# Spreading the rows of B over the partitions by transfers and a ScalarE copy instead of by TensorE

## The chip, the cores and the metric

The kernel runs on one core of one Trainium2 chip. The core has five engines that work side by side[...]: TensorE (PE, the matrix multiplies), VectorE (DVE), ScalarE (ACT), GpSimd (POOL) and SyncE (SP), which here issues nearly all transfers. Transfers move data between the HBM and the on-chip memory SBUF; matmuls write to PSUM, which VectorE and ScalarE can read and write[...]. The metric is the device time of one execution in microseconds (us), the median over runs; less is better.

## What is computed

The input is a batch of four images of 48 x 48 positions with 128 channels. Layer 0 normalizes, projects to 256 inner channels, convolves, and runs four selective scans over the 2304 positions (row order, column order, and both reversed). Layer 1 is an attention followed by a spectral convolution (called STU below). Only the scan matters for the change:

```python
def step(h, inp):
    dt_l, u_l, B_l, C_l = inp
    dA = jnp.exp(dt_l[..., None] * A)
    h = h * dA + (dt_l * u_l)[..., None] * B_l[:, :, None, :]
    y = jnp.einsum('bkdn,bkn->bkd', h, C_l)
    return (h, y)
```

The state `h` has 256 channels times 16 state entries for each image and direction. `B_l` and `C_l` are 16 numbers for each position, the same for all channels: whoever forms the product `(dt*u)*B` on the chip needs each row of B repeated on all the partitions that hold a channel of that state entry.

## The kernel before, in words

**Stages.** A prologue prepares image 0. Then, for each image, comes a scan stage, and after it an epilogue with the attention, in which the next image's prologue is done as well. The STU of image b-1 runs inside the scan stage of image b, as TensorE work between the pieces of the scan; in the scan stage of image 0 there is no such STU, and the mixing of its weights (`mixture`) takes its place. The STU of the last image runs alone at the end.

**The scan stage.** Four directions k times six chunks of 384 positions (`CS`) make 24 chunks for each image. A chunk has eight units `(h, q)`: h is one of two halves of the channels, q one of four groups of four state entries. A unit is laid out as 128 partitions (four state entries times 32 channels) by four channel groups by 384 positions. For each unit:

- `spread` (L439) makes the rows of B stand on all 128 partitions, 32 partitions for each of the four state entries.
- `enter` (L445) multiplies `dt*u` by them: one instruction over 128 x 1536 elements. Three of eight units (`POOLED`, L484) do this on GpSimd, the other five on VectorE.
- `scan` (L452), four times: ScalarE computes `exp` into a PSUM tile `dA` (two buffers), VectorE scans with it.
- `times_c` (L461): GpSimd multiplies by C, and `sum_c` (L469) sums over the state entries by TensorE; `add_y` (L478) adds to the result on VectorE.

**Two ways to spread B before the change.** A unit on VectorE has its B made by a matmul of the chunk's `xd` (which holds the projected rows of B) with a constant matrix `spread` of zeros and ones, into the one PSUM tile of pool `psB` (tag "B"). A unit on GpSimd[...] its B comes to SBUF by `Chunk.fetch` (L423): four transfers of 48 KB, each reading one row of B from HBM (`xdd`) for 32 partitions. The rows of C come in the same way (fetch indices 4 to 7). `FETCHED` (L489) lists the fetched indices: 1, 3 and 4 to 7. Each fetched index has one SBUF buffer `bc`, which is refilled for the next chunk by `refill` (L542) once the second half (h = 1) of the current chunk has read it.

**Order of the work.** The order is written out by hand: `scans` (L509) emits, for each unit s, the instructions of all engines, and each engine executes its own in that order. Within step s the order is: `enter` (which multiplies for unit s+1 on VectorE or unit s+2 on GpSimd), preparation of later chunks, scan of group 0, STU or mixing work, `times_c` of unit s-1, scan of group 1, preparation, STU work, `spread(s + 2)`, scan of group 2, STU work, preparation, scan of group 3, refills, `sum_c` of unit s-2, STU work. `more` hands out the STU work in proportion to the matmul columns done so far (`done`), out of a total in which `CHUNK_COLS` (L491) are counted for each chunk of the scan.

**Preparation of a chunk** (`prep`, L342) starts 17 units before the chunk and also uses the tile "B" of `psB` for its matmuls (`xp` L368, `dt` L380); ScalarE reads those results at L373 and L383. Its softplus (L391) needs another table of functions than `exp`, so ScalarE loads a table before it and another one after it. It falls in the step of the last unit of a chunk (s mod 8 = 7), just before `spread(s + 2)`.

**The STU** multiplies at L969 (`cv`), copies one result in three to SBUF on ScalarE (`Q`, L983), adds the others to it on VectorE (`U`, L994) and multiplies by weights at L1031 (`pr`). Its Toeplitz tiles `tt` are fetched at L942.

Of the kernel before, what the change touches and what calls it, by code (L numbers as in the profile page):

```python
# [8 lines left out]
F32 = mybir.dt.float32  # L9
AF = mybir.ActivationFunctionType  # L10
ALU = mybir.AluOpType
# [4 lines left out]
P = 128  # L16
# [5 lines left out]
CS = 384  # L22
SUB = 384
NT = L // P
G4, DL, C4, Q4 = 4, 32, 4, 4
# [29 lines left out]
def hybrid_kernel(ctx: ExitStack, tc: tile.TileContext, a: dict, out: bass.AP):  # L55
# [3 lines left out]
    nc = tc.nc  # L59
    ctx.enter_context(tc.manual_schedule())  # L60
    wp = ctx.enter_context(tc.tile_pool(name="w", bufs=1, side="left"))
# [30 lines left out]
    for h in range(NH):  # L92
# [14 lines left out]
                            fill=0.0, base=0, channel_multiplier=1)  # L107
    nc.gpsimd.affine_select(gmean, gmean, pattern=[[4, C // 4], [0, 4]], compare_op=ALU.is_ge,
                            fill=0.0, base=3, channel_multiplier=-1)
# [5 lines left out]

    onerow = wp.tile([P, 1], F32, name="onerow")
    nc.vector.memset(onerow, 0.0)

    spread = wp.tile([P, 2, Q4, C4, DL], F32, name="spread")
    nc.vector.memset(spread, 0.0)  # L120
    for v in range(2):
        nc.gpsimd.affine_select(onerow, onerow, pattern=[[0, 1]], compare_op=ALU.not_equal, fill=1.0,
                                base=-R - 64 * v, channel_multiplier=1)
        nc.gpsimd.affine_select(spread[:, v], spread[:, v], pattern=[[-C4, Q4], [-1, C4], [0, DL]],
                                compare_op=ALU.not_equal, fill=1.0, base=-32 - 64 * v, channel_multiplier=1)

    csum = wp.tile([P, DL], F32, name="csum")
    nc.vector.tensor_reduce(csum, ident.rearrange("p (c j) -> p j c", j=DL), AX.X, ALU.add)
# [302 lines left out]
    class Unit:  # L431
# [7 lines left out]
        def spread(self, ps):  # L439

            self.bt = ps.tile([P, 512], F32, tag="B", name=f"B{self.name}")
            nc.tensor.matmul(self.bt[:, :CS], spread[:, self.ch.k // 2, self.q].rearrange("p c j -> p (c j)"),  # L442
                             self.ch.xd, start=True, stop=True)

        def enter(self, pool):  # L445

# [37 lines left out]
    POOLED = ((0, 3), (1, 1), (1, 3))  # L484
    order = [(k, c) for k in range(K) for c in (range(NCH) if k < 2 else reversed(range(NCH)))]
    quads = [(h, q) for h in range(NH) for q in range(Q4)]
    STEPS = 15
    LEAD = 17
    FETCHED = sorted({q for h, q in POOLED} | set(range(Q4, 2 * Q4)))  # L489

    CHUNK_COLS = (len(quads) - len(POOLED)) * CS + len(quads) * CS + 3 * CS  # L491

    def begin_scans(b, pool):

        chunks = [Chunk(b, k, c) for k, c in order]
        preps = [ch.prep(pool) for ch in chunks]
        for i in range(3 * STEPS):
            if next(preps[0]) is not None:
                yield
        for i in FETCHED:  # L500
            chunks[0].fetch(i, pool)
        for i in range(3 * (LEAD - len(quads))):
            if next(preps[1]) is not None:
                yield
        for i in range(3 * (LEAD - 2 * len(quads))):
            next(preps[2])
        yield chunks, preps

    def scans(b, chunks, preps, front, sp, back, work, work_cols):  # L509

        units = [Unit(ch, h, q) for ch in chunks for h, q in quads]
        total = len(chunks) * CHUNK_COLS + work_cols
        done = [0]

        def more(share):

            while done[0] < share * total:
                cols = next(work, None)
                if cols is None:
                    break  # L520
                done[0] += cols

        def enter(s):

            if s + 2 < len(units) and units[s + 2].pool:
                units[s + 2].enter(sp.s)
            if 0 <= s + 1 < len(units) and not units[s + 1].pool:
                units[s + 1].enter(sp.s)

        def spread(s):  # L530
            if s < len(units) and not units[s].pool:
                units[s].spread(back.psB)
                done[0] += CS

        def prepare(s):

            ci, j = divmod(s, len(quads))
            for c in range(ci + 1, ci + 4):
                if c < len(chunks) and 0 <= s - len(quads) * c + LEAD < STEPS:
                    done[0] += next(preps[c]) or 0  # L540

        def refill(s, i):  # L542

            if 0 <= s < len(units) and s // len(quads) + 1 < len(chunks):
                u, nxt = units[s], chunks[s // len(quads) + 1]
                if u.h == NH - 1:
                    nxt.fetch(i + u.q, front)

        pending = []
        spread(0)  # L550
        enter(-2)
        enter(-1)
        spread(1)
        for s in range(len(units) + 2):
            real = s < len(units)
            enter(s)
            prepare(s)
            if real:
                units[s].scan(0, back.psa)
            more((s + 0.25) / len(units))  # L560
            if 1 <= s <= len(units):
                units[s - 1].times_c()
            if real:
                units[s].scan(1, back.psa)
            if pending:
                pending.pop().add_y()
            prepare(s)
            more((s + 0.5) / len(units))
            spread(s + 2)
            if real:  # L570
                units[s].scan(2, back.psa)
            more((s + 0.75) / len(units))
            prepare(s)
            if real:
                units[s].scan(3, back.psa)
            refill(s - 3, Q4)
            if s + 1 < len(units) and units[s + 1].pool:
                refill(s + 1, 0)
            if s >= 2:
                units[s - 2].sum_c(back.psy)  # L580
                done[0] += CS
                if units[s - 2].q == Q4 - 1:
                    pending.append(units[s - 2])
            more((s + 1) / len(units))
        for u in pending:
            u.add_y()
        assert next(work, None) is None
# [528 lines left out]
    once.close()  # L1116
    front = Stage(tc, "f0", "left", one=(1, SB), xd=(3, SB), rep=(3, SB))
    first = begun(begin_scans(0, front))
    begin0.close()
    start_y(0)  # L1120
    for b in range(B):
# [3 lines left out]
        if b == 0:  # L1125
            mixed = Stage(tc, "m", "right", two=(2, SB))
            scans(b, *first, front, sp, ps, mixture(mixed, ps), MIX_COLS)
            mixed.close()
        else:
            scans(b, *first, front, sp, ps, stu_alone(b - 1, ps), STU_COLS)  # L1130
# [29 lines left out]
        if more:  # L1160
            front = Stage(tc, f"f{b + 1}", "left", one=(1, SB), xd=(3, SB), rep=(3, SB))
            pieces = begin_scans(b + 1, front)
# [67 lines left out]
```

## Time and profile before

Time before: 6410.29 us, the median of three runs from 6404.66 to 6411.98 us. The profiled execution spans 6421.2 us.

| Engine | busy, us | share of the span | instructions |
|---|---|---|---|
| PE | 5440.6 | 85% | 25032 |
| DVE | 4823.6 | 75% | 6193 |
| POOL | 3842.7 | 60% | 1825 |
| ACT | 2800.0 | 44% | 5053 |

The first queue of transfers (q1) moved 1025.00 MB. The instructions that the change touches, from the profile's groups:

| Line, engine | what | count | busy, us | mean, ns |
|---|---|---|---|---|
| L442 PE | matmul into B (two passes each) | 960 | 443.0 | 546 |
| L450 DVE | multiply by B from PSUM | 480 | 832.2 | 1734 |
| L450 POOL | multiply by B from SBUF | 288 | 994.2 | 3452 |
| L455 ACT | exp into dA | 3072 | 1782.0 | 585 |
| L429 SP | transfers of rows of B and C, 48.0 KB each | 2304 | 3.4 to landing | |

How to read it: a share of the span is an average over stages that have different limits. The part of the profile that divides the span into 40 slices shows the four scan stages as the stretches in which VectorE's digit is 9. A wait is given with the engine and the line that ended it. Idle time of an engine that doesn't set the end costs nothing.

### The profile page before, as it was taken

To read this page: it belongs to the slowest core of one execution; us is meant where nothing else is said; L and a number is where in the kernel's file an instruction comes from. 1 tells how busy PE (TensorE), PEld (TensorE's weight loads), DVE (VectorE), ACT (ScalarE), POOL (GpSimd) and SP (SyncE) were. 2 spreads that over 40 slices of the span, in tenths; PEclk is the share of its full clock that TensorE was granted. 3 is DMA by queue.
4 is the path that set the end of the run, shared out by engine and by line. 5 is a ranking of instruction groups with operands and counts; after the bars stand their busy time and mean duration, and the time that the engine had idled before them with its cause. 6 is when DMAs were issued, how large, how long until landed. Compare 5 with 4: busy or idle time off the path is not lost.

```text
span 6421.2 us, 75575 instructions
## 1 busy us (share of the span) xinstructions
PE 5440.6 (85%) x25032; PEld 3353.1 (52%) x25032; DVE 4823.6 (75%) x6193; ACT 2800.0 (44%) x5053; POOL 3842.7 (60%) x1825
## 2 busy tenths in 40 slices
PE   3656555697999998888999999788999999789999
PEld 1222222444556566544556567544555567547789
DVE  6999999548999998558999998458999999322111
ACT  2555555244555554244555554244555554221000
POOL 1989888406778887306788887207788888100000
PEclk6787777799999999899999999899999999899999
DMA  4556566126878889127878889127788888025546
GB/s 104 139 138 151 139 144 148 40 55 162 199 196 215 216 221 247 59 62 165 198 195 217 222 218 256 39 64 179 189 203 215 219 224 246 28 67 151 154 141 212
DMA packets 658246, 1033.52 MB, mean 161 GB/s; under 512 B 93856, under 2 KB 515872, under 8 KB 633120
## 3 DMA queue, kind: packets, MB, share of 16 engines
q1 hardware_dynamic: 652032, 1025.00, 62.3%
q10 hardware_dynamic: 5824, 3.69, 0.3%
q8 instruction: 200, 3.28, 0.2%
q14 instruction: 190, 1.56, 0.1%
HBM read 905.79 MB, written 122.56 MB: 160 GB/s over the span
## 4 chain that ended last, share of the span: by engine, by line
PE 45%; DVE 24%; DMA 16%; POOL 4%; issue 4%; ACT 4%; SPq 3%; DVEq 0%; ACTq 0%; POOLq 0%
PE cv L969 19%; DVE s L458 11%; PE pr L1031 6%; DVE s L450 5%; DMA tt<-fd 5%; DMA rep<-dtdud 4%; PE s L714 4%; PE y L475 3%; PE o L707 3%; DMA bc<-xdd 3%; POOL s L467 3%; PE op L650 2%; PE B L442 2%; DVE xc L264 2%; DVE re L408 2%
## 5 line engine op out<-in xcount | busy, mean ns | idle before, releaser
L467 POOL TENSOR_TENSOR s<-s,bc 128x1536 f32<-128x1536 f32 x768 | 2647.8, 3449 | 179.8 <-DVE s L458 88.9
L458 DVE TENSOR_TENSOR_SCAN s<-dA,carry,s 128x384 f32<-128x384 f32 x2560 | 2458.1, 1000 | 190.1 <-ACT dA L455 189.0
L455 ACT ACTIVATE dA<-rep,A 128x384 f32<-128x384 f32 x3072 | 1782.0, 585 | 1627.0 <-DVE s L458 1622.2
L969 PE MATMUL cv<-tt,u 128*128 128x256 f32 (+3 forms) x7680 | 1632.6, 351 | 64.3 <-DVE U L994 38.0
L969 PEld LDWEIGHTS cv<-tt,u 128*128 128x128 f32 x7680 | 1259.7, 190 | 583.1 <-issue 266.1
L450 POOL TENSOR_TENSOR s<-rep,bc 128x1536 f32<-128x1536 f32 x288 | 994.2, 3452 | 95.3 <-DMA bc<-xdd 95.3
L969 PE MATMUL cv<-tt,us 128*128 128x256 f32 (+3 forms) x3840 | 841.0, 358 | 106.6 <-DVE U L994 55.3
L994 DVE TENSOR_TENSOR U<-cv,Q 128x256 f32<-128x256 f32 (+1 forms) x1280 | 480.3, 381 | 596.0 <-PE cv L969 581.2
L450 DVE TENSOR_TENSOR s<-rep,B 128x1536 f32<-128x1536 f32 x480 | 832.2, 1734 | 56.1 <-PE B L442 32.8
L475 PE MATMUL y<-s,csum 128*32 128x384 f32 x6144 | 720.6, 544 | 142.4 <-DVE ya L481 85.0
L969 PEld LDWEIGHTS cv<-tt,us 128*128 128x128 f32 x3840 | 639.7, 195 | 323.8 <-DVE U L994 89.7
L1031 PE MATMUL pr<-U,G 128*128 128x512 f32 (+4 forms) x2048 | 694.7, 469 | 3.5 <-DVE U L994 3.2
L983 ACT COPY Q<-cv 128x256 f32<-128x256 f32 (+3 forms) x640 | 224.0, 351 | 1027.2 <-PE cv L969 1025.5
L442 PE MATMUL B<-xd,spread 128*128 128x384 f32 x960 | 443.0, 546 | 177.4 <-DVE s L450 166.8
L458 DVE TENSOR_TENSOR_SCAN s<-dA,s 128x384 f32<-128x384 f32 x512 | 459.3, 938 | 70.9 <-ACT dA L455 70.7
L466 POOL COPY carry<-s 128x4 f32<-128x4 f32 x640 | 121.6, 190 | 574.8 <-DVE s L458 534.5
L1031 PEld LDWEIGHTS pr<-U,G 128*128 128x128 f32 x2048 | 334.5, 190 | 198.2 <-issue 137.0
L714 PE MATMUL s<-xnT 128*128 128x512 f32 (+1 forms) x720 | 357.9, 582 | 42.7 <-ACT xnT L676 23.4
L475 PEld LDWEIGHTS y<-s,csum 128*32 128x32 f32 x6144 | 127.7, 112 | 497.4 <-issue 336.3
L158 POOL TENSOR_TENSOR ln_vu<-ln_vu,mhalf 128x4 f32<-128x4 f32 (+1 forms) x20 | 26.8, 1341 | 602.0 <-DVE ln_vu L157 602.0
L716 ACT ACTIVATE e<-s,shift 128x512 f32<-128x512 f32 (+1 forms) x360 | 231.2, 644 | 314.1 <-PE s L714 313.6
L707 PE MATMUL o<-e,xn 128*128 128x512 f32 (+1 forms) x720 | 343.4, 560 | 4.5 <-ACT e L716 4.5
(157 smaller groups left out, 3638.1 us busy)
## 6 DMA issues: line engine op xcount, KB each, us to landing
rep<-dtdud SPq DMA_DIRECT2D x768, 384.0 KB, 7.8
tt<-fd SPq DMA_DIRECT2D x192, 577.0 KB, 5.5
bc<-xdd SPq DMA_DIRECT2D x2304, 48.0 KB, 3.4
tt<-fd SPq DMA_DIRECT2D x192, 513.0 KB, 4.5
tt<-fd SPq DMA_DIRECT2D x192, 385.0 KB, 4.3
dtdud<-re SPq DMA_DIRECT2D x768, 96.0 KB, 2.3
G<-gd SPq DMA_DIRECT2D x192, 256.0 KB, 5.3
tt<-fd SPq DMA_DIRECT2D x64, 514.0 KB, 5.6
```

The costliest lines, as they stand in the source:

```text
L442: nc.tensor.matmul(self.bt[:, :CS], spread[:, self.ch.k // 2, self.q].rearrange("p c j -> p (c j)"), self.ch.xd, start=True, stop=True)
L450: eng.tensor_tensor(s, self.ch.rep[self.h][:, 1], bt.unsqueeze(1).to_broadcast([P, G4, CS]), ALU.mult)
L455: nc.scalar.activation(dA[:, :CS], ch.rep[self.h][:, 0, g], AF.Exp, scale=A[:, ch.k, self.h * G4 + g, self.q:self.q + 1])
L458: nc.vector.tensor_tensor_scan(s, dA[:, CS - 1::-1] if ch.rev else dA[:, :CS], s, 0.0 if ch.first else carry[:, self.h, self.q, g:g + 1], ...
L467: nc.gpsimd.tensor_tensor(self.s, self.s, ch.bc[Q4 + self.q].unsqueeze(1).to_broadcast([P, G4, CS]), ALU.mult)
L475: nc.tensor.matmul(ch.y[g * DL:(g + 1) * DL, :CS], csum, self.s[:, g], start=(self.q == 0), stop=(self.q == Q4 - 1))
L707: nc.tensor.matmul(po[J][:, :w], xn[:, i], e[:, :w], start=(i == 0), stop=(i == NT - 1))
L714: nc.tensor.matmul(p[:, :w], xnT[:, i * P:(i + 1) * P], xnT[:, 512 * J:512 * J + w], start=True, stop=True)
L716: nc.scalar.activation(e[:, :w], p[:, :w], AF.Exp, bias=shift)
L969: nc.tensor.matmul(p2[:, :, at - first:], x, t[:, :, hi - 1 - at + J * P:end if end >= 0 else None:-1], start=(J == 0), stop=(J == nb - 1))
L994: nc.vector.tensor_tensor(dst, src, q, ALU.add)
L1031: nc.tensor.matmul(p[:, :, :v], Gs[n][:, q, x, :], U[n][:, 4 * q:4 * q + 4, :v], start=False, stop=(k == KF - 1 and q == 1 and v == w))
```

## The change

The five units in eight that multiply on VectorE no longer get their B from TensorE. All four groups of rows of B are fetched by transfers (fetch indices 0 to 7 instead of 1 and 3 to 7), and ScalarE copies the fetched tile from SBUF to the PSUM tile "B", from which VectorE multiplies as before. The copy stands in the order where the matmul stood. The constant matrix `spread` goes. The refill of a row group of B is emitted in every step (it acts only for units with h = 1), no longer only before a unit of GpSimd, and the columns of the spreading matmuls are taken out of the count by which the STU work is handed out. The purpose is to take the spreading off TensorE, which also carries the STU.

```diff
-    spread = wp.tile([P, 2, Q4, C4, DL], F32, name="spread")
-    nc.vector.memset(spread, 0.0)
...
-        nc.gpsimd.affine_select(spread[:, v], spread[:, v], pattern=[[-C4, Q4], [-1, C4], [0, DL]],
-                                compare_op=ALU.not_equal, fill=1.0, base=-32 - 64 * v, channel_multiplier=1)
...
         def spread(self, ps):
 
             self.bt = ps.tile([P, 512], F32, tag="B", name=f"B{self.name}")
-            nc.tensor.matmul(self.bt[:, :CS], spread[:, self.ch.k // 2, self.q].rearrange("p c j -> p (c j)"),
-                             self.ch.xd, start=True, stop=True)
+            nc.scalar.copy(self.bt[:, :CS], self.ch.bc[self.q])
...
-    FETCHED = sorted({q for h, q in POOLED} | set(range(Q4, 2 * Q4)))
-
-    CHUNK_COLS = (len(quads) - len(POOLED)) * CS + len(quads) * CS + 3 * CS
+
+    CHUNK_COLS = len(quads) * CS + 3 * CS
...
-        for i in FETCHED:
+        for i in range(2 * Q4):
             chunks[0].fetch(i, pool)
...
                 units[s].spread(back.psB)
-                done[0] += CS
...
             refill(s - 3, Q4)
-            if s + 1 < len(units) and units[s + 1].pool:
-                refill(s + 1, 0)
+            refill(s + 1, 0)
```

## The prediction

> **What bounds the kernel now.** I read the 40 slices first. VectorE is at 9 in four stretches, the scan stages; TensorE is at 9 in the last three of them too, and the transfers' row at 7 to 9.
>
> ```profile
> PE   3656555697999998888999999788999999789999
> DVE  6999999548999998558999998458999999322111
> DMA  4556566126878889127878889127788888025546
> ```
>
> Only the scan stages hold what changes, so I asked for the busy time by window: the first scan stage and the second, from first scan to last (the third and fourth are 1127.5 and 1128.6 us), then the second cut at the starts of its chunks 8, 20 and 23. Columns: length, then busy time of PE, PEld, DVE, ACT, POOL, granted TensorE clock, share and rate of transfers.
>
> ```profile
> 124.78:1168.17 1043.39, 614.05 (x2652) 245.49 (x2652) 949.49 (x978) 597.30 (x1078) 923.42 (x423) 0.77 0.59 141
> 1471.49:2605.32 1133.83, 1047.89 (x5347) 662.26 (x5347) 1054.13 (x1303) 584.19 (x1051) 925.79 (x422) 0.98 0.83 209
> ...
> 1471.50:1872.70 401.20, 362.93 (x1586) 204.95 (x1586) 361.92 (x462) 204.57 (x374) 305.94 (x143) 0.97 0.79 190
> 1872.70:2406.10 533.40, 511.16 (x2480) 319.91 (x2480) 520.69 (x620) 292.14 (x510) 465.96 (x213) 0.99 0.86 217
> 2406.10:2563.10 157.00, 136.94 (x986) 108.58 (x987) 131.60 (x171) 68.59 (x130) 117.36 (x58) 0.93 0.92 244
> ```
>
> In the first stage VectorE is 91% busy and TensorE 59%. In the others both are at 92 to 93%, but not evenly: in the middle twelve chunks VectorE works 98% of the time, in the first eight both have 10% idle, and in chunks 20 to 22 the transfers are at 0.92. The change takes nothing from VectorE, so it can win only VectorE's idle time: 94 us in the first stage (1043.4 - 949.5), 80 in the second (1133.8 - 1054.1), 74 and 73 in the others. The lists of waits by window say what ends it. First stage, then the first eight chunks of the second, then its middle twelve (us in total, times, longest):
>
> ```profile
> DVE s L458 <- ACT dA L455: 66.3, 42, 16.4
> DVE s L450 <- PE B L442: 15.3, 7, 3.4
> DVE s L450 <- issue: 12.6, 4, 4.5
> ...
> ACT Q L983 <- PE cv L969: 75.5, 53, 9.5
> DVE s L458 <- ACT dA L455: 35.8, 31, 3.5
> ...
> DVE s L458 <- ACT dA L455: 11.3, 17, 1.5
> ```
>
> The first stage waits for B itself. (The four "issue" waits stand before the same multiply; the timeline shows one at 430.04, TensorE having stood 6.8 us for the weights `M` with the B matmul queued behind.) Later VectorE waits for `dA`, hence for ScalarE. Following each such gap back through ScalarE's records: in the first eight chunks ScalarE was mostly late from standing at a `Q` copy whose `cv` TensorE had not finished (some 25 of the 36 us); most of the rest lies behind the table loads around softplus.
>
> **What the Trainium skill says.** "ScalarE: Activation LUTs", section "What ACT_TABLE_LOAD costs", gives 186 ns + 0.833 ns per element for an instruction with immediate operands; for 384 elements an estimate of 506 ns. The trace has 472 ns for the copy of the same shape out of PSUM (L383). The page's 1283 ns for a table load is the trace's figure exactly. "DMA: Bandwidth & Descriptors", section "Issuing engines are not separate DMA queues", says that all transfers share 16 engines; so the added ones compete with `tt` and `rep`, and the 0.92 above shows where. "TensorE: Matmul & The Clock Gate", Part 1, says idle windows lower the clock: in this trace 0.77 at 59% busy against 0.98 at 92%. Lighter TensorE work may thus be paced a little slower.
>
> **The change part by part.**
>
> *TensorE loses the B matmuls*: 443.0 us over 480, so 0.92 us each and 111 us per stage. TensorE in stages two to four falls from 1048 to 937 us. This is worth time only where VectorE waited for TensorE. First stage: 26 us of B waits within the stage (15.3 + 12.6, less 1.7 before the first scan) go. First eight chunks of each later stage: 25 + 3 us (direct waits for `cv`) hang on TensorE. Five matmuls a chunk take 8 x 5 x 0.92 = 37 us from its 363, so it is nearer 85% busy than 90%; the middle chunks run well with TensorE at 96%, so I take 20 of the 28 as won. Middle: 1 us. Chunks 20 to 22 wait for transfers: 2 us.
>
> *ScalarE gains 480 copies*. Bounds are 472 ns (L383) and 585 ns (the `exp` of the same shape from SBUF to PSUM); I take 472, since no pointer operand is read. That is 57 us per stage, 584 to 641 of some 1125: no new bound, but ScalarE works in order, and behind the copy stand the `exp` of groups 2 and 3, for which VectorE waits. The copy needs its row group landed and the tile "B" read by the multiply of unit s+1. That multiply precedes the scan of group 0, whose end the next `exp` awaits anyway, so the second wait is normally covered. I laid a copy of 472 ns, record by record, into the gap before the third `exp` of each unit concerned (118 a stage), starting after ScalarE's previous record and that multiply. What the slack before the scan doesn't take up is 15.6, 18.0, 17.8 and 18.0 us by stage (22 to 23 with 600 ns). Most of it is certain: in the step of softplus the copy lies in an already late chain, here ScalarE's, then VectorE's record:
>
> ```profile
> 1567.19 1.28 ACT L391 ACT_TABLE_LOAD   x1
> 1568.48 0.84 ACT L391 ACTIVATE re<-re 128x768 f32<-128x768 f32 x1
> ...
> 1571.06 1.28 ACT L455 ACT_TABLE_LOAD   x1
> 1572.35 0.58 ACT L455 ACTIVATE dA<-rep,A 128x384 f32<-128x384 f32 x1
> ...
> 1572.97 1.02 DVE L458 TENSOR_TENSOR_SCAN s<-dA,carry,s 128x384 f32<-128x384 f32 x1 [1.63 <-ACT dA L455]
> ```
>
> 24 such steps at up to 0.47 make 11 us a stage. Of the second stage's 18, 9 fall in the first eight chunks (where an earlier `cv` gives back a third: I count 6), 8 in the middle, 2 in the end.
>
> *Transfers gain* two row groups of four transfers in each of 96 chunks: 768 of 48 KB, 37.7 MB on 1033.5. SyncE issues eight more per chunk at 0.42 us, 3.4 of some 47. The row group is fetched three steps (some 17 us) before its copy, against 3.4 us median and 13.7 at most to landing; the row group of unit 3 has the same lead today and GpSimd waited for it only at the start. So the landing costs nothing later. At the end of a stage, 24 x 49 KB = 1.2 MB at 244 GB/s would cost 4.8 us where the transfers are full; I count 3.
>
> *Start of the first stage*: the first B is now behind the `rep` transfers. In the timeline VectorE multiplies at 119.6 and GpSimd's row group lands at 129.8; a delay of 8 us, of which a gap of 16.4 us at 149.96 (TensorE waiting for `M`) takes some: 4.
>
> *Edits at nothing*: the constant `spread` and its fills lie in the prologue beside the loading of weights. Removing the columns from the count leaves the STU's mean pace as it was, hidden behind VectorE.
>
> Sum: first stage -26 + 16 + 4 = -6. Later stages: first eight chunks -20 + 6 = -14; middle -1 + 8 = +7, less 2 for copies that a `U` add on VectorE covers, +5; end -2 + 2 + 3 = +3, less 2 where a `cv` wait takes the copy in; together some -8, three times -24. In all -30: 6380 us.
>
> **The rivals.**
>
> *VectorE becomes the sole bound.* If all waits for TensorE go, the first eight chunks fall to VectorE's 362 us + 10 behind tables + 4 for copies = 376, -25; with +6 in the middle and nothing at the end, -19 a stage, -57; the first stage -25. 6328 us. For: the middle's 98%. Against: waits for a first `tt` stay.
>
> *ScalarE's copies take the place of the waits (slower).* If lighter TensorE work wins nothing in the later stages, the 69 us of copies (15.6 + 18.0 + 17.8 + 18.0), 14 for transfers (3 x 4.8), and 4 at the start stand against 26: +61, 6471 us. For: a stall of VectorE in the middle is lost for good. Against: the 25 us behind `cv` in the first eight chunks.
>
> *The two cancel*: won and lost some 60 us each, 6405 us, within 0.2%.
>
> **How the numbers follow.** The likeliest case, 6380, has 0.52; VectorE sole bound 0.14; cancelling 0.13; slower 0.21. Faster by over 0.2% (12.8 us): 0.14 + 0.47 of the first, 0.61. Same: 0.13 + 0.05, 0.18. Slower: 0.21. The range runs from 6310, below the second case since the shift of STU pieces may move each later stage by some us, to 6450, where half of the slower case is out.
>
> **What would show it.** Right: the B waits of the first stage gone; the first eight chunks of a later stage 10 to 20 us shorter with TensorE near 85%; the middle 4 to 8 us longer; the gap after softplus 0.4 us longer; chunks 20 to 22 unchanged or a little longer. Wrong: copies that wait for `bc` transfers, the middle longer by over 15 us, or the first eight chunks unmoved.

## The result, and the profile after

| | median, us | lowest to highest | runs |
|---|---|---|---|
| before | 6407.48 | 6402.20 to 6411.98 | 4 |
| after | 6465.19 | 6459.20 to 6476.28 | 4 |

The ratio is 1.0092, 95% interval 1.0075 to 1.0110: the change costs 58 us, where 30 us of gain were predicted.

The 40 slices of the kernel after, in the rows that were shown of before:

```profile
PE   3555555788988988788988888788988888789999
DVE  6999999458999998458999997459999998322111
DMA  4666666027888889128888888127878888025546
```

In the scan stages of images 1 to 3 TensorE is now mostly at 8, where it was at 9, and the transfers went from 7 to 8 in some slices. VectorE's row is hardly changed, as it has the same work. The windows of the four scan stages, first scan to last (length; busy time of PE, PEld, DVE, ACT, POOL; clock; share and rate of transfers):

```profile
130.71:1156.08 1025.37, 550.11 (x2416) 215.94 (x2416) 949.57 (x977) 642.17 (x1197) 922.11 (x423) 0.67 0.62 152
1456.39:2604.76 1148.37, 997.61 (x5109) 628.35 (x5109) 1054.23 (x1303) 631.39 (x1170) 924.64 (x422) 0.95 0.85 215
2903.45:4054.76 1151.31, 1005.50 (x5110) 634.44 (x5111) 1053.79 (x1303) 631.34 (x1170) 924.82 (x422) 0.94 0.85 214
4354.30:5506.77 1152.47, 1004.51 (x5110) 632.59 (x5111) 1052.86 (x1303) 630.86 (x1170) 924.87 (x422) 0.94 0.84 214
```

Against before the first stage is 18 us shorter (1043.4 to 1025.4), the others 15, 24 and 24 us longer (from 1133.8, 1127.5 and 1128.6), the first scan is 6 us later. VectorE's busy time is within 3 us of before in every stage, so nearly all of it is idle time: in the second stage 94 us in place of 80. (These windows are of the two profiled executions, whose spans are 41 us apart; the one of before is a longer one, so the timed 58 us is the better figure of the whole.)

The second stage cut as before, at the starts of its chunks 8 and 20:

```profile
1456.39:1856.40 400.01, 349.11 (x1510) 192.43 (x1510) 361.49 (x463) 222.00 (x415) 305.92 (x143) 0.95 0.82 200
1856.40:2399.70 543.30, 484.52 (x2364) 303.94 (x2365) 521.46 (x620) 314.95 (x571) 465.50 (x213) 0.97 0.87 219
2399.70:2604.90 205.20, 164.12 (x1240) 132.12 (x1242) 171.29 (x222) 94.44 (x185) 153.23 (x68) 0.92 0.84 231
```

The first eight chunks gained 1 us and not 14, the middle twelve lost 10 and not 5, the end lost 6 (199.2 us before) and not 1. In the third stage the same parts are 394, 547 and 210 us against 401, 533 and 194.

Which engine was late? TensorE's list of waits in the second stage, before and then after (line numbers are those of each kernel, so the same line can have two):

```profile
PE cv L969 <- DVE U L994: 31.4, 27, 3.9
PE cv L969 <- DMA tt<-fd: 17.2, 5, 5.1
```

```profile
PE cv L960 <- DVE U L985: 65.6, 49, 4.6
PE cv L960 <- DMA tt<-fd: 47.5, 12, 7.5
```

TensorE, which was relieved, waits longer: for `U`, which VectorE makes, and for `tt`, the Toeplitz tiles of the STU, which the change doesn't touch. In the order of the program a late `tt` makes a late `cv`, then a late `Q` copy on ScalarE, then a late `dA`. `tt` is issued by SyncE. SyncE's own list of waits over the whole span, before and then after:

```profile
SPq L942 <- PE cv L969: 1152.3, 454, 13.3
...
SPq L429 <- DMA rep<-dtdud: 287.6, 222, 2.8
...
SPq L942 <- DMA rep<-dtdud: 103.0, 76, 2.9
```

```profile
SPq L933 <- PE cv L960: 687.9, 298, 13.2
SPq L424 <- DMA rep<-dtdud: 551.3, 410, 2.6
...
SPq L933 <- DMA rep<-dtdud: 177.6, 137, 2.5
```

The first line of each is a good wait: SyncE that waits for TensorE to free a buffer of `tt` is ahead. That wait shrank by 464 us. In its place stand more waits of a row of B or C, or of `tt`, for a `rep` transfer, with which it shares no data.

The cause is a limit in how the program issues: SyncE's transfers use eight semaphores in turn (763 to 766 transfers on each in the kernel after), and one that comes to a semaphore waits until the transfer eight places earlier has landed. In the second stage every wait of SyncE for a landing, 249 us before and 349 after, was for the transfer just eight places earlier. A `rep` transfer has 384 KB and took 7.7 us to land (median), so a short transfer eight places behind it stands still, and everything queued behind that too. SyncE's timeline in the middle of the second stage, after:

```profile
2015.19 2.19 SPq L424 DMA_DIRECT2D bc<-xdd  x4
2019.02 0.38 SPq L933 DMA_DIRECT2D tt<-fd  x1
2020.77 4.08 SPq L424 DMA_DIRECT2D bc<-xdd  x4
2024.95 0.38 SPq L933 DMA_DIRECT2D tt<-fd  x1
```

Columns are start, length, line and how many are merged. Four rows take 1.8 us where nothing holds them; here, from 2020.77 on, 4.08: the second of them could go at 2022.62, when the `rep` transfer that was issued eight places earlier, at 2014.30, had landed. Adding up SyncE's records in the second stage gives this account (worked out from the trace: issuing, waits that a landing ended, waits that an engine ended). The waits for an engine are SyncE's slack.

| kernel | transfers | issuing, us | waits for a landing, us | waits for an engine, us | stage, us |
|---|---|---|---|---|---|
| before | 1239 | 569 | 249 | 268 | 1134 |
| after | 1427 | 644 | 349 | 110 | 1148 |

The 188 added transfers took 75 us to issue, and the waits for landings grew by 100 us; the slack paid for most of it, and less than half was left. (In the first stage the slack fell from 484 to 313 us, and there the change is no loss.)

The added rows are late too. ScalarE's list over the whole span, after:

```profile
ACT B L437 <- DMA bc<-xdd: 53.1, 23, 14.3
```

One of these waits, of 14.3 us, stands before the first scan; 12 to 14 us fall in each of the last three stages. The rows that a copy waited for there had been issued 2 to 8 us before ScalarE came to the copy, and most took 7 to 9 us to land.

This is the theory that the experiments test: **the added transfers fill SyncE's queue, `tt` is issued late, and TensorE, ScalarE and VectorE are late in turn.** The rivals: the copies on ScalarE cost the time; the bytes do; the count by which STU work is handed out does.

### The profile page after: what moved, and what is told of

It reads as the page before. It is cut to its first block, busy times and chain, and to the rows that moved or that the text cites. A ratio compares the mean times of both kernels' runs of the same rounds, so it can differ in the third digit from the quotient of the medians.

```text
span 6461.8 us, 75336 instructions
## 1 busy us (share of the span) xinstructions
PE 5226.2 (81%) x24072; PEld 3232.2 (50%) x24072; DVE 4820.7 (75%) x6192; ACT 2988.1 (46%) x5533; POOL 3836.8 (59%) x1823
## 4 chain that ended last, share of the span: by engine, by line
PE 34%; DVE 26%; DMA 24%; SPq 5%; ACT 4%; issue 4%; POOL 3%; DVEq 0%; ACTq 0%; POOLq 0%
PE cv L960 15%; DVE s L452 13%; DMA rep<-dtdud 9%; DMA tt<-fd 7%; DMA bc<-xdd 6%; DVE s L444 5%; PE pr L1022 4%; PE s L705 3%; PE o L698 3%; POOL s L461 2%; PE op L641 2%; SPq L424 2%; PE y L469 2%; DMA G<-gd 2%; DVE xc L259 2%
## 5 line engine op out<-in xcount | busy, mean ns | idle before, releaser
L960 PE MATMUL cv<-tt,u 128*128 128x256 f32 (+3 forms) x7680 | 1668.0, 361 | 241.2 <-DVE U L985 130.8
L960 PEld LDWEIGHTS cv<-tt,u 128*128 128x128 f32 x7680 | 1290.5, 197 | 722.1 <-issue 284.9
L444 POOL TENSOR_TENSOR s<-rep,bc 128x1536 f32<-128x1536 f32 x288 | 993.5, 3450 | 123.2 <-DMA bc<-xdd 105.6
L469 PE MATMUL y<-s,csum 128*32 128x384 f32 x6144 | 744.9, 561 | 245.6 <-POOL s L461 130.4
L444 DVE TENSOR_TENSOR s<-rep,B 128x1536 f32<-128x1536 f32 x480 | 832.3, 1734 | 19.2 <-ACT B L437 19.2
L1022 PE MATMUL pr<-U,G 128*128 128x512 f32 (+4 forms) x2048 | 707.9, 477 | 6.7 <-DMA G<-gd 3.4
L824 PE MATMUL G<-M,W 128*128 128x128 f32 (+2 forms) x768 | 244.6, 464 | 136.6 <-DMA M<-in_M_phi_plus 94.9
```

The lines of the kernel that those rows point to most:

```text
L444: eng.tensor_tensor(s, self.ch.rep[self.h][:, 1], bt.unsqueeze(1).to_broadcast([P, G4, CS]), ALU.mult)
L469: nc.tensor.matmul(ch.y[g * DL:(g + 1) * DL, :CS], csum, self.s[:, g], start=(self.q == 0), stop=(self.q == Q4 - 1))
L824: nc.tensor.matmul(p[:, :n] if j else p[:, NF - 1 - i], W[:, q if t else 0, i], M[t][:, i].unsqueeze(1).to_broadcast([P, n, C]) if j else ...
L960: nc.tensor.matmul(p2[:, :, at - first:], x, t[:, :, hi - 1 - at + J * P:end if end >= 0 else None:-1], start=(J == 0), stop=(J == nb - 1))
L1022: nc.tensor.matmul(p[:, :, :v], Gs[n][:, q, x, :], U[n][:, 4 * q:4 * q + 4, :v], start=False, stop=(k == KF - 1 and q == 1 and v == w))
```

## The experiments

### One part at a time: the copy without the transfers

const_copy keeps the copies and the count edit, but copies a constant tile and fetches only what was fetched before.

```diff
+    cst = wp.tile([P, CS], F32, name="cst")
...
-            nc.scalar.copy(self.bt[:, :CS], self.ch.bc[self.q])
+            nc.scalar.copy(self.bt[:, :CS], cst)
...
-        for i in range(2 * Q4):
+        for i in FETCHED:
```

> The copies alone: ScalarE copies a constant tile of the same shape into the tile B, and the transfers are those of the kernel before (the multiplication by B is therefore by a constant). If the added transfers hold up SyncE's queue and with it the tt tiles (transfers theory): 6375 to 6410 us, stages two to four at most 1130 us each. If ScalarE's copies delay the exp (copies theory): 6450 to 6475 us, as the changed kernel.

Measured: 6397.58 us, ratio 0.9971 (0.9958 to 0.9983). Without the added transfers the change is a small gain. Its stages are 1030.6, 1132.0, 1129.5 and 1129.3 us (the second 2 us over what the transfers theory allowed), and SyncE's waits for an engine are 249 us in the second, near the 268 of before. The transfers cost the difference of the two ratios, 1.0092 - 0.9971 = 0.0121, some 78 us. In the two profiled executions they start the first scan 8 us later, shorten the first stage by 5 and lengthen the others by 16, 22 and 23.

TensorE's list in the second stage of const_copy:

```profile
PE cv L964 <- DVE U L989: 74.4, 55, 5.2
PE cv L964 <- DMA tt<-fd: 27.1, 8, 7.9
```

The long waits for `U` are here too, so they don't come from the added transfers; the waits for `tt` are what rises with these, from 27.1 to 47.5 us. VectorE's waits in this stage rise by 11 us, 9 of them for `dA` (63.4 to 72.4). That the late `tt` and the late rows make these 9 us is the reading of the lists; no run changes the lateness of `tt` alone.

### The transfers without the copy

fetch_more is the kernel before, with the two added row groups fetched into a buffer that nobody reads. fetch_small brings an eighth of each such row.

```diff
-            t = self.bc[i] = pool.one.tile([P, CS], F32, tag=f"bc{i}", name=f"bc{self.name}_{i}")
+            t = self.bc[i] = pool.one.tile([P, CS], F32, tag="bcx" if i in (0, 2) else f"bc{i}", name=f"bc{self.name}_{i}")
...
-    FETCHED = sorted({q for h, q in POOLED} | set(range(Q4, 2 * Q4)))
+    FETCHED = range(2 * Q4)
...
-            if s + 1 < len(units) and units[s + 1].pool:
-                refill(s + 1, 0)
+            refill(s + 1, 0)
```

and for fetch_small, on top of that:

```diff
-                nc.sync.dma_start(t[c * DL:(c + 1) * DL], src[row].partition_broadcast(DL))
+                n = 48 if i in (0, 2) else CS
+                nc.sync.dma_start(t[c * DL:(c + 1) * DL, :n], src[row, :n].partition_broadcast(DL))
```

> The transfers alone: the kernel before with the 768 added transfers of rows of B, which nobody reads (both row groups go into one buffer). Transfers theory: 6430 to 6480 us, with SyncE waiting less for TensorE and TensorE more for tt. Copies theory: 6400 to 6415 us.

> As the kernel with the added transfers alone (6510 us), but each added transfer brings 48 of 384 columns: the same number of transfers, an eighth of their bytes. If the number counts, by the time SyncE needs to issue one and by the eight that it keeps under way (slots theory): 6475 to 6515 us. If the bytes count (bytes theory): 6420 to 6440 us.

Measured: fetch_more 6510.04 us, ratio 1.0144 (1.0126 to 1.0163); fetch_small 6474.98 us, ratio 1.0094 (1.0079 to 1.0109), against 6415.7 and 6414.3 us for the kernel before. The first is 30 us above the range of the transfers theory, the second at the lower edge of the slots theory. Transfers that nobody waits for cost the old kernel 0.0144, some 92 us. An eighth of the bytes still costs 0.0094, two thirds of it: in the kernel before, most of the cost is their number, and a third goes with their bytes. SyncE's list of waits in fetch_more, whole span:

```profile
SPq L941 <- PE cv L968: 713.5, 301, 13.4
SPq L429 <- DMA rep<-dtdud: 584.7, 435, 3.1
```

It is the list of the kernel after, in a kernel that spreads B by TensorE.

### Fewer transfers with the same bytes

pairs_b is the changed kernel, with the rows of B for two values of q in one transfer (24 transfers a chunk in place of 32, as many as before the change); pairs_all pairs the rows of C as well (16 a chunk).

```diff
+            t = pool.one.tile([P, 2, CS], F32, tag=f"bc{i}", name=f"bc{self.name}_{i}")
+            self.bc[i], self.bc[i + 1] = t[:, 0], t[:, 1]
...
+                row = src[64 * (self.k // 2) + 32 + 4 * i + c]
+                nc.sync.dma_start(t[c * DL:(c + 1) * DL],
+                                  bass.AP(row.tensor, row.offset, [[0, DL], [4 * CS, 2], [1, CS]]))
```

> The changed kernel with the rows of B for two q brought by one transfer: 24 transfers a chunk in SyncE's queue, as before the change, instead of 32, with the bytes of the changed kernel. Slots theory: 6395 to 6425 us, near the kernel with copies of a constant (6398). Bytes theory: 6450 to 6475 us.

> As the run before, and the rows of C in pairs too: 16 transfers a chunk. Slots theory: 6370 to 6405 us, below the kernel before. Bytes theory: 6450 to 6475 us. Rows of C are fetched later relative to their use, so GpSimd may wait for them; by over 60 us in all it would show in its row for the product with C.

Measured: pairs_b 6428.57 us, ratio 1.0029 (1.0017 to 1.0040); pairs_all 6414.48 us, ratio 1.0003 (0.9995 to 1.0012). With the bytes unchanged, 768 transfers less take back 0.0063 of the 0.0121, and 1536 less take back 0.0089. Both times lie above the range of the slots theory (by 4 and 9 us), and further below that of the bytes theory. Not all comes back, and pairs_all isn't below the kernel before: a pair lands later (median 8.5 us in pairs_b, 6.0 in pairs_all, against 3.8 for a row in the kernel after), and ScalarE's copies waited 64.3 us for rows in pairs_all, 53.1 in the kernel after.

The account of SyncE in the second stage, for these kernels and the two before:

| kernel | transfers | issuing, us | waits for a landing, us | waits for an engine, us | stage, us | third and fourth stage, us |
|---|---|---|---|---|---|---|
| const_copy | 1243 | 569 | 257 | 249 | 1132 | 1130, 1129 |
| fetch_more | 1423 | 643 | 362 | 98 | 1157 | 1157, 1158 |
| fetch_small | 1423 | 645 | 337 | 106 | 1140 | 1147, 1138 |
| pairs_b | 1243 | 569 | 327 | 189 | 1138 | 1133, 1142 |
| pairs_all | 1059 | 496 | 349 | 250 | 1132 | 1141, 1138 |

With the count edit in (after, const_copy and the pairs), the second stage gets shorter as the slack grows: 110, 189, 250 and 249 us go with 1148, 1138, 1132 and 1132. The later stages follow this only in part: the third and fourth of pairs_all have the slack of const_copy (247 and 237 us against 244 and 253) and take some 10 us more. So slack isn't the whole account; the waits for landings stay long in pairs_all. fetch_more and fetch_small, without the edit, have the slack of after, and their stages are to be held against before: 23 and 6 us longer than its 1134 in the second, 29 and 20 longer in the third (1156.6 and 1147.2 against 1127.5).

### The same transfers from another engine

gp_queue is the changed kernel, with the added row groups issued by GpSimd.

```diff
-                nc.sync.dma_start(t[c * DL:(c + 1) * DL], src[row].partition_broadcast(DL))
+                eng = nc.gpsimd if i in (0, 2) else nc.sync
+                eng.dma_start(t[c * DL:(c + 1) * DL], src[row].partition_broadcast(DL))
```

> The changed kernel with the added transfers issued by GpSimd instead of SyncE: the same bytes, the same number, but not in SyncE's queue. Slots theory: 6390 to 6430 us, SyncE waiting for TensorE again as before. Bytes theory: 6450 to 6480 us. GpSimd's own time for issuing could add to either, seen as a busier GpSimd.

Measured: 6527.45 us, ratio 1.0177 (1.0162 to 1.0192): slower than the change itself, where the theory wanted 6390 to 6430. SyncE was relieved as foreseen (waits for an engine 221 us in the second stage). But there is a new price. From the lists by line, GpSimd, then VectorE (busy us, mean ns | idle before):

```profile
L425 POOL DMA_DIRECT2D bc<-xdd x768 | 385.8, 508 | 65.5 <-DMA xdd<-xd 65.3
```

```profile
L403 DVE TENSOR_TENSOR re<-re,xc 128x384 f32<-128x384 f32 x192 | 203.6, 1101 | 79.3 <-DMA bc<-xdd 40.3 <-ACT re L386 38.9
```

An issue on GpSimd occupies it for 508 ns, 386 us in all, and the median landing is 7.2 us. L403 is a multiply on VectorE with both inputs in SBUF; in the kernel after its mean is 735 ns, here 1101, so 192 x 0.366 = 70 us more on VectorE. It isn't the issuing beside it that makes it long: the 121 of the 192 that met no GpSimd instruction took 677 ns on the mean, as in the kernel after (179 of them, 679 ns), and the 44 that ran beside GpSimd's multiply by C alone took 2487 ns (13 in the kernel after, 1509 ns). The two multiplies meet more often now; that this comes from GpSimd being held up by its issues is likely, not shown.

47 of the 55 us between the two profiled executions lie in the first stage, where GpSimd is busy 1015 us of 1072, in place of 922 of 1025. In the three later stages VectorE's busy time rose by 14, 15 and 10 us and its idle time fell by 7, 12 and 13, some two thirds of what the added transfers had put on it (11, 18 and 20 us against const_copy). So with SyncE relieved most of the added idle time goes, which agrees with the theory, but the time as a whole went the other way: this way out costs more than it saves.

### The count alone

uncounted is the kernel before with one part of the change: the columns of the spreading matmuls are taken out of the count (the even count). count_pooled turns the count round: columns are counted in the steps whose unit two ahead is multiplied by GpSimd. after_counted is the changed kernel with the old count.

```diff
-    CHUNK_COLS = (len(quads) - len(POOLED)) * CS + len(quads) * CS + 3 * CS
+    CHUNK_COLS = len(quads) * CS + 3 * CS
...
                 units[s].spread(back.psB)
-                done[0] += CS
```

> The count alone: the kernel before, with the columns of the B matmuls left out of the count that hands out the STU work. Both theories: 6400 to 6420 us. Above 6430 us the shifted STU pieces themselves would be a cause.

> The kernel before, with its matmuls that spread B, but with the count turned round: CS columns are counted in the steps whose unit two ahead is a pooled one (it has no spreading matmul) and none in the steps that do spread. Three eighths of the steps then draw fewer matmuls of the work beside the scans, the other five more. Theory (the period of VectorE in which the multiply of the unit two ahead is one of its own is long, the other short, so matmuls of work belong in the long ones): a further gain over the even count's 6371.8 us, 6335 to 6365 us, ratio 0.988 to 0.9925. Rival one (the even count is best, since TensorE then has the spreading matmul and too many matmuls of work in the same step): 6380 to 6420 us. Rival two (only the total counted matters, not the step): 6365 to 6378 us.

> The changed kernel with the old count of columns kept (each copy still adds CS columns to the count, and the columns of a chunk are the old sum). It tests whether the count edit also helps in the changed kernel, where no matmul spreads B any more. Theory (the count is a saving of its own, since counted columns draw the matmuls of work into the short steps of VectorE and away from the long ones): without it the loss is larger by about the 44 us that the count alone gave to the kernel before, 6495 to 6520 us. Rival one (in the changed kernel SyncE sets the pace and TensorE's placing is hidden): 6460 to 6475 us, as the changed kernel. Rival two (the count must tell the truth: the count edit helps the kernel before by chance, and with the copies a wrong count in either direction costs the same): 6475 to 6490 us.

Measured: uncounted 6371.84 us, ratio 0.9936 (0.9921 to 0.9951). The edit that I had costed at nothing is a gain of 0.0064, some 41 us, in all four stages (the last two are 1114.9 and 1119.0 us), the first two being:

```profile
124.45:1151.72 1027.27, 637.53 (x2652) 265.56 (x2652) 954.50 (x978) 595.04 (x1070) 922.21 (x423) 0.75 0.60 143
1454.51:2573.04 1118.53, 1046.24 (x5347) 661.66 (x5347) 1051.38 (x1303) 585.82 (x1052) 925.20 (x422) 0.98 0.84 212
```

Stage by stage 16, 15, 13 and 10 us less than before, with the same instructions on every engine. I took VectorE's idle time by the step in which it falls (second stage, mean of 24 chunks, from the trace): in step 5 it fell from 0.82 to 0.30 us and in step 1 from 0.58 to 0.34, while in step 0 it rose from 0.16 to 0.42. A step is counted here from its first scan to the first scan of the next. Steps 1, 3 and 5 hold no multiply by B of VectorE's own and are short (4.7, 4.0 and 4.9 us before, against 6 to 8 for the long ones; step 3 had next to no idle time to lose). With B counted, a step that spreads B gets less STU work and a step that doesn't gets more, so the reading is that the short steps 1 and 5 got more than TensorE could do in them.

count_pooled was to carry this further: 6377.16 us, ratio 0.9934 (0.9920 to 0.9949), no better than the even count, and in the range of its rival two, that the step doesn't matter. The wait moved: in the second stage, step 6 rose from 0.21 to 0.65 us. So that the even count helps is shown; that each shift toward the long steps helps is refuted, and that the steps are why the even count helps is not shown. after_counted: 6495.06 us, ratio 1.0117 (1.0100 to 1.0134), against 1.0092 (1.0075 to 1.0110) with the edit; step 5 has 1.14 us of idle time there, 0.54 with the edit. By these ratios the edit is worth some 0.0025 in the changed kernel, less than half of what it is worth before, though the time lies at the edge of what its theory said. The intervals overlap; its size there stays uncertain.

### The copy earlier

In pairs_all_early the copy stands ahead of the softplus step, not behind it.

```diff
+            spread(s + 2)
             prepare(s)
             more((s + 0.5) / len(units))
-            spread(s + 2)
```

> pairs_all with one edit more: the copy of a unit's B is put ahead of the prepare step in the middle of a unit, so that it no longer stands behind the softplus step on ScalarE. Theory (the copy behind the softplus step is what is left of the cost of the copies: VectorE's idle time in that step rose by about 0.4 us, 0.4 us x 96 = 38 us a run): 6370 to 6395 us, ratio 0.993 to 0.997. Rival (the copies come soon enough, what is left is TensorE's waits and the copies' time on ScalarE that delays the exponentials): 6405 to 6420 us, no change against pairs_all.

Measured: 6485.05 us, ratio 1.0108 (1.0093 to 1.0123), some 67 us slower than pairs_all; both expectations fail. ScalarE's waits for the multiply that frees the one PSUM tile "B", first in pairs_all, then in pairs_all_early:

```profile
ACT B L447 <- DVE s L454: 55.3, 51, 1.8
```

```profile
ACT B L447 <- DVE s L454: 169.2, 151, 1.8
```

And what that delays, in ScalarE's timeline of pairs_all_early at the end of a chunk:

```profile
1574.98 0.48 ACT L447 COPY B<-bc 128x384 f32<-128x384 f32 x1 [1.45 <-DVE s L454]
1575.48 1.28 ACT L386 ACT_TABLE_LOAD   x1
1576.77 0.84 ACT L386 ACTIVATE re<-re 128x768 f32<-128x768 f32 x1
```

In the order of the change, softplus and its table load run while VectorE multiplies; here the copy waits 1.45 us for that multiply, and softplus stands behind it. VectorE's idle time in this step (mean of the second stage's chunks) rose from 1.37 us in pairs_all to 2.33. Of the two, the place that the change gave the copy is the better one.

### Without any spreading

no_spread lets VectorE multiply by a constant SBUF tile: no matmul, no copy, no added transfer. It was to give the bound of what can be won.

```diff
-            self.bt = ps.tile([P, 512], F32, tag="B", name=f"B{self.name}")
-            nc.scalar.copy(self.bt[:, :CS], self.ch.bc[self.q])
+            self.bt = cst
```

> Neither matmul nor copy nor added transfers: VectorE multiplies by a constant tile in SBUF (B is left out). Both theories give the gain from a lighter TensorE here, with nothing paid for it: 6340 to 6385 us. The difference to the kernel with copies of a constant is the price of the copies: transfers theory 5 to 35 us, copies theory 70 us or more. At or above 6400 us would say that TensorE's B matmuls cost nothing.

Measured: 6879.93 us, ratio 1.0723 (1.0707 to 1.0739), far above what both theories said. The least work gives the slowest kernel. Lists by line, VectorE, then GpSimd:

```profile
L445 DVE TENSOR_TENSOR s<-rep,cst 128x1536 f32<-128x1536 f32 x480 | 1451.9, 3025 | 2.5 <-DMA rep<-dtdud 2.5
```

```profile
L445 POOL TENSOR_TENSOR s<-rep,bc 128x1536 f32<-128x1536 f32 x288 | 1152.6, 4002 | 93.3 <-DMA bc<-xdd 93.3
L461 POOL COPY carry<-s 128x4 f32<-128x4 f32 x640 | 560.3, 876 | 366.5 <-DVE s L453 346.7 <-PE cv L963 4.2 <-DMA tt<-fd 3.0
```

The same multiply took 1734 ns with its second input in PSUM, GpSimd's 3450 and the carry copy 189. The Trainium skill has this in "SBUF — State Buffer", section "Who interferes with whom": a VectorE instruction with two SBUF inputs contends with a GpSimd instruction that reads SBUF, and the other stands still meanwhile. The trace agrees: the 117 multiplies of VectorE that met no multiply of GpSimd took 1.73 us on the mean, as with PSUM, and the others up to 4.99. 1291 ns more for each of 480 multiplies is 620 us of VectorE, of which its lower idle time takes a part back. So this run gives no bound for the change, but it shows what the copy to PSUM is for: it spares VectorE and GpSimd this, where a multiply straight from the fetched rows would have two SBUF inputs.

### A kernel that beats both

matmul_pairs keeps the spreading matmul, takes its columns out of the count, and brings the rows of C in pairs (16 transfers a chunk in place of 24).

```diff
-                done[0] += CS
...
-            refill(s - 3, Q4)
+            refill2(s - 2, Q4)
```

(`refill2` and the paired transfer are those of pairs_all, for C alone.)

> A version meant to beat both: the kernel before with the matmuls that spread B kept, the spreading columns no longer counted, and the rows of C for two values of q brought by one transfer (16 transfers a chunk in place of 24, the same bytes). Theory (SyncE's slots are a cost already in the kernel before, where 250 us of a late stage are waits for one of the eight under way): somewhat below the even count's 6371.8 us, 6340 to 6368 us, ratio 0.9885 to 0.993. Rival (the kernel before has slack on SyncE, 255 us in a late stage, so fewer transfers buy nothing): 6368 to 6380 us. If the pairs land too late for ScalarE and GpSimd: above 6380 us.

Measured: 6354.88 us, ratio 0.9904 (0.9878 to 0.9930), within its theory's range; by the two ratios to the kernel before it is 1.9% below the changed kernel (0.9904 / 1.0092 = 0.981). SyncE's waits for an engine in the second stage rise to 351 us (issuing 503, landings 219). Whether the pairing adds to the count edit isn't settled: 0.9904 (0.9878 to 0.9930) and 0.9936 (0.9921 to 0.9951) overlap. Where SyncE has slack, as before the change, fewer transfers buy little, if anything.

## Why the prediction was wrong

The ratios split the change into three parts: the count edit 0.9936 - 1 = -0.0064 (-41 us), the copy in place of the matmul 0.9971 - 0.9936 = +0.0035 (+22 us), the transfers 1.0092 - 0.9971 = +0.0121 (+78 us). They sum to the measured +59 us by construction, and the first two depend on the order: with the count edit taken last (after_counted) it is -16 us, and the copy in place of the matmul some -3. fetch_more is an independent measure of the third (+92 us on the old kernel). Of the -30 us forecast, the transfers had +13 (9 at the ends of the stages, 4 at the start), the count 0, and the copy in place of the matmul the rest, -43. So in the first order two terms were missed by 65 us each: the transfers, and the copy for the matmul, where the gain from a lighter TensorE didn't come (in the other order this one was missed by 40). The count hid a part of it.

- **Transfers, the first step that failed.** "So the landing costs nothing later", and at the end "I count 3". I priced the transfers by bytes against 16 engines, and by issue time, "eight more per chunk at 0.42 us, 3.4 of some 47". The issue time was right: 75 us over 24 chunks is 3.1. What I left out is that SyncE issues in order, one transfer after the other, with 249 us of waits for landings already in a stage of 1134; of the 47 us of a chunk, issuing took 24 and waits for landings 10, so only some 11 were slack. And the lead was not the 17 us that I took from the order of the program: the rows that copies waited for were issued 2 to 8 us before ScalarE came to them, so the copies waited for `bc`, which I had named as a sign of being wrong. The list of SyncE's waits was there to be read. I leaned on the Trainium skill's "DMA: Bandwidth & Descriptors", section "Issuing engines are not separate DMA queues", for what transfers share; the same section says that the time on the sequencer is "usually small relative to the DMA itself". For one transfer that agrees (0.42 us against 3.8 to landing); for the sum it doesn't here, where issuing takes 644 of 1148 us.
- **The count, costed at nothing.** "Removing the columns from the count leaves the STU's mean pace as it was, hidden behind VectorE." The STU still ends with its stage; what moved is the pace inside a chunk, and it is worth -41 us in the old kernel and some -16 in the changed one. Without this gain, which I didn't foresee, the miss would have been larger.
- **First eight chunks, the second step that failed: "I take 20 of the 28 as won".** With the copies, 14 were to be left; won was 1 us in the second stage and 8 in each of the others, and a part of that can be the count edit's, which alone won 6, 12 and 11 there. TensorE did become lighter (363 to 349 us busy in the second stage), but then waited: for `U` 74.4 us in const_copy, where the kernel before had 31.4, so what was taken off TensorE became waiting for VectorE, and with the added transfers more for `tt`. In the second stage the sign of being wrong that I gave, first eight chunks unmoved, is what came.
- **TensorE "falls from 1048 to 937 us".** It fell to 998 in the second stage, though 238 matmuls are gone. The records of matmuls overlap (the groups of this stage add up to 1160 us before, where TensorE was busy 1048), so a group's busy time isn't what the engine's busy time loses; and the clock went from 0.98 to 0.95 (`cv` by `u` took 364 ns in place of 353 in that stage). The lower clock was foreseen, without a size. const_copy has the same 998 us at 0.96 with no added transfers.
- **The copies' own time: right.** 474 ns each against 472 taken. The gap behind softplus grew by 0.37 us (1.00 to 1.37, mean of the step) against 0.4 foreseen. The copy in place of the matmul is +22 us net, or some -3 by the other order, where my terms gave -43; the runs don't separate the cost of the copies from the gain of a lighter TensorE.
- **First stage: right in kind, the size in part by luck.** The B waits are gone, VectorE waits only for `dA`, 75.8 us in place of 66.3. With 18 us gained and 6 lost at the start it is -12, where -6 was said. But the count edit alone took 16 us off this stage in the kernel before. With the old count kept (after_counted) the stage gained 11 and started 6 later, -5.
- **The slower rival**, 6471 us, is 6 us from the result, by luck, for its terms were others: it had 14 us for transfers and nothing for the count, where the runs show 78 and -41.

What stays open: how the 78 us divide between late `tt`, late copies and the bytes beyond the third that fetch_small shows, since fetch_small leaves the old kernel's other waits in place; why a relieved TensorE comes to wait so much longer for `U`; and why the two ways of counting in uncounted and count_pooled come out alike.

## What to carry to other kernels

Before moving work from an engine to transfers, make the account of the engine that issues them: issuing time, waits for landings, and waits for other engines in the stage concerned; only the last is slack, and here short transfers behind long ones ate it by their number more than by their bytes. An edit to what a planner counts is an edit to the schedule and needs a run by itself. When an instruction is moved ahead in an in-order engine, look first at what frees its output buffer, since all behind it will wait for that too.

## What the hardware showed that I had not expected

- A VectorE multiply of 128 x 1536 with its second input in SBUF took 3025 ns beside a busy GpSimd, 1734 ns with it in PSUM, and GpSimd's carry copies went from 189 to 876 ns.
- Transfers issued by GpSimd took it 508 ns each and landed in 7.2 us (SyncE's took 0.42 us and landed in 3.8 in the kernel after). A multiply on VectorE with both inputs in SBUF took 0.68 us with no GpSimd instruction beside it and 2.5 us beside GpSimd's multiply by C, in the same run.
- With eight semaphores in turn, all of SyncE's 349 us of waits for landings in a stage were for the transfer eight places earlier; none was for data.
- Two rows in one transfer landed in 6.0 us (pairs_all) or 8.5 (pairs_b) against 3.8 for one, so pairing saved issuing but delivered each row later.
